# Finer interleaving of output products with attention, GpSimd's output work ordered after the causal masks, transposes one product later, and a third chain bank in an adaLN transformer block

## The chip, the core and the metric

The kernel runs on one core of one Trainium2 chip. The metric is device time in microseconds (us) for one execution. The core has five engines that run side by side, each through its own queue in order: TensorE (PE in the profile, with its weight loads as PEld) multiplies matrices into the accumulator memory PSUM, VectorE (DVE) and ScalarE (ACT) work element by element and can read PSUM, GpSimd (POOL) works element by element on the on-chip memory SBUF, and SyncE (SP) mostly issues DMA transfers. They wait for each other through semaphores.

## The reference

One adaLN-modulated transformer block in float32 on x of shape (2, 1024, 1024): two sequences ("batches"), 1024 tokens, model width 1024, 32 heads of 32, feed-forward width 2752.

```
mod = silu(c) @ wmod -> sa, ca, ga, sb, cb, gb          # |ga|, |gb| at least 0.25
h = layernorm(x) * (1 + ca) + sa
q, k, v = clip(h @ Wqkv.T, -8, 8)                       # then a layernorm over q and over k
scores = q k^T / sqrt(32) + slope_h * (pos_k - pos_q)   # causal
x = x + ga * (softmax(scores) v) @ Wout.T
h = layernorm(x) * (1 + cb) + sb
x = x + gb * ((silu(h Wg^T * ag) * (h Wu^T * au)) Wd^T * ad)
```

## The kernel before, in words

**Products in seven.** All large products use a Strassen-Winograd scheme on 2 x 2 blocks: seven block products in place of eight. For a pair of token tiles `j` (2 x 128 tokens), `seven` (L832) issues P1, P2, U2, P5, U3, P53, U6 in this order, each with four matmuls of 128x128 weights and 512 columns. (A float32 matmul shows as two records in the profile.) The operands are blocks (A11, ..) and sums of blocks (S1 to S4 of the tokens, T1 to T4 of the weights). S1 and S2 are made on VectorE, S3 and S4 on GpSimd (`sums_a`, L778); T1 and T2 on VectorE, T3 and T4 on GpSimd (L822 to L827). The seven go through two PSUM banks x and y, the chain: P1 goes into x, is copied out by ScalarE, and U2, U3 and U6 accumulate on it there; P2 goes into y and is read by VectorE, then P5 starts y anew, is copied out, and P53 accumulates on it. Each of P2, P53, U3 and U6 finishes a quarter of the result, which `read` takes out of the bank.

`Banks` (L745) hands out the banks. `pair` swaps x and y from one set of seven to the next. `turn` gives the next of the other banks for a transpose or a row-sum product. Where only one other bank is there, `fresh` says whether a step of the product has gone by since the last turn. In batch 0's projections there are four other banks, after that one.

**Between the matmuls.** After each `grain` matmuls `seven` yields, and the callback `between` may issue waiting pieces of work (`Todo`, L873): a layernorm's second half first, then transposes by TensorE of normalized token tiles (`turned`, L853: four 128x128 transposes into a bank, then copies out of it by VectorE, in batch 0's projections and the last output tiles shared with ScalarE), each with a `turn` of the banks. `places(q0, n)` says from which product on (`q0`) and how many at a place (`n`) transposes may go.

**Stages.** (1) The modulation vectors and batch 0's projections for q, k and most of v (`projections`, L943). Here a scheduler that estimates times may reorder TensorE's instructions. (2) Attention over both batches, with the rest as filler between its steps: the end of batch 0's v, batch 1's projections, then the output products of batch 0 and of batch 1's first half (`output`, L1265). From here on TensorE keeps the program's order (`pinned`), while the order on the other engines is still the scheduler's. (3) The output products of batch 1's second half, alone. (4) The feed-forward: gate and up products, then down products.

**Attention** (`attention`, L1022) goes through units of one group of four heads, one block of 512 queries and one block of 128 keys. `scores` issues four matmuls into four PSUM banks, ScalarE takes their exponentials (L1080), and where the key block touches the diagonal GpSimd zeroes what lies above it (the mask, `affine_select`, L1084). `weigh` multiplies with v two units later (`LAG`), and VectorE or GpSimd add the exponentials up (L1112). A `settle` makes row sums with a matrix of ones in one of the other banks (L1123, L1130). The four score banks are there once only, so the next unit's scores wait for this unit's exponentials.

**The weave.** `together` (L1157) takes attention's steps one by one and after each issues filler until the filler's share, by rough costs (`MM` = 0.9 us a matmul), stands level with attention. So the grain of the filler sets how finely the two are woven: it is 4 matmuls in batch 0's projections, 2 in batch 1's, and 2 in the output products.

**Output** works for each pair of token tiles on operands that `operand` (L1221) prepares during the product before: the attention result times the reciprocal row sums (L1246, half on VectorE and half on GpSimd), S1 and S2 on VectorE, S3 and S4 on GpSimd (L1250, L1251). `read` scales the result by ga (on GpSimd L1312, else VectorE) and adds it to x on GpSimd (L1313). Then comes the layernorm, the store of x by SyncE (L1320), the transposes, and `token_operands` (L1194), two of whose four subtractions are GpSimd's (L1201, L1202).

**The layernorm** (`normalize`, L696) takes statistics on VectorE, then 1/sqrt(var + eps) as exp(-0.5 ln) on ScalarE with one Newton step in tiny VectorE operations (L711, L719 to L722), and at last applies it (L724). `behind(a, b)` adds no wait: it tells the scheduler to put a after b.

Of the kernel before, what the change touches and what calls it, by code (L numbers as in the profile page):

```python
# [12 lines left out]
FP = mybir.dt.float32  # L13
# [6 lines left out]
P = 128  # L20
# [460 lines left out]
def kernel(  # L481
# [211 lines left out]
    last_exp = [None]  # L693
    last_mask = [None]

    def normalize(tiles, outs, small, nm):  # L696
# [12 lines left out]
        def rest_():  # L709
            ve = small.tile([P, n], FP, tag="ve", name=f"ve_{nm}")  # L710
            nc.vector.tensor_scalar_add(ve, mv[:, :, 1], EPS)  # L711
            lv = small.tile([P, n], FP, tag="lv", name=f"lv_{nm}")
            ln = nc.scalar.activation(lv, mv[:, :, 1], AF.Ln, bias=eps_t)
            if last_exp[0] is not None:
                behind(ln, last_exp[0])
            rstd = small.tile([P, n], FP, tag="rstd", name=f"rstd_{nm}")
            nc.scalar.activation(rstd, lv, AF.Exp, scale=-0.5)
            fix = small.tile([P, n], FP, tag="fix", name=f"fix_{nm}")
            nc.vector.tensor_mul(fix, rstd, rstd)  # L719
            nc.vector.tensor_mul(fix, fix, ve)  # L720
            nc.vector.tensor_scalar(fix, fix, -0.5, 1.5, ALU.mult, ALU.add)
            nc.vector.tensor_mul(rstd, rstd, fix)  # L722
            for m, (t, o) in enumerate(zip(tiles, outs)):
                nc.vector.tensor_scalar(o, t, mv[:, m, 0:1], rstd[:, m : m + 1], ALU.subtract, ALU.mult)  # L724
# [20 lines left out]
    class Banks:  # L745

        def __init__(self, two, others):
            self.two, self.others = two, others  # L750
            self.at = self.nt = self.made = 0
            self.seen = -1
            self.spare = None

        def pair(self):
            if self.spare is not None:
                x = self.two[self.at]
                self.two[self.at], self.spare = self.spare, x
            else:
                self.at ^= 1  # L760
            return self.two[self.at], self.two[1 - self.at]

        def fresh(self):
            return len(self.others) > 1 or self.made != self.seen

# [66 lines left out]
    def seven(a, bt, banks, read, between, grain):  # L832

        x, y = banks.pair()
        for c_, qa, qb_, q in SEVEN:
            bank = x if c_ == "x" else y
            first = q in ("P1", "P2", "P5")
            for j in range(KC // 2):
# [9 lines left out]
            banks.made += 1  # L848
            yield grain * MM
# [88 lines left out]
    def projections(b, pools, banks, places, extra=None, other=None, side=lambda n, e: None):  # L938
# [8 lines left out]
        for part in range(3):  # L947
            bt = weights_b(wp_, wqkv_t[:, ts(part, D)], f"{b}_{part}", wt_dram[part], other, b == 0 and part == 1)
            for j in range(NT // 2):
# [16 lines left out]
                part_t = {}  # L966
                q0, n = (2 - b, places) if b or part or j else (5, 4)

# [225 lines left out]
    def token_operands(b, j, h2, pool):  # L1194
# [24 lines left out]
    def operand(b, j, ap_):  # L1219
# [25 lines left out]
        for m, kh, q, eng in blocks:  # L1245
            eng.tensor_mul(a[q], a[q], rb[:, ds(kh * 4, 4), ts(m, P)])  # L1246
# [3 lines left out]
        nc.gpsimd.tensor_sub(a["S3"], a["A11"], a["A21"])  # L1250
        nc.gpsimd.tensor_sub(a["S4"], a["A12"], a["S2"])  # L1251
        made[b, j] = a
# [11 lines left out]

    def output(b, js, pools, banks, bt, todo, keep, q0=1, after=None):  # L1265

# [8 lines left out]
        for j in js:  # L1275
# [24 lines left out]
            def read(q, bank):  # L1300
# [9 lines left out]
                else:  # L1310
                    nc.vector.tensor_add(yg, yg, bank)
                    nc.gpsimd.tensor_mul(yg, yg, ga[:, ts(n, HALF)])  # L1312
                nc.gpsimd.tensor_add(xs[m][:, ts(n, HALF)], xs[m][:, ts(n, HALF)], yg)  # L1313
# [56 lines left out]
    with ExitStack() as st:  # L1370
# [77 lines left out]
        for us in dense0:  # L1448
            if us == "mark":
                break  # L1450
        banks.others = banks.others[0:1]
        banks.nt = 0
# [110 lines left out]
    def first_tokens():  # L1563
        ost.close()
        mid.close()
        banks.others.append(banks.spare)
        token_tiles((1, 0, 2, 3, 4, 6, 5))

    banks.spare = late_pools.enter_context(
        tc.tile_pool(name="spare_ps", bufs=1, space=PSUM, side="right")  # L1570
    ).tile([P, 512], FP, name="spare_ps")
    alone(output(1, range(NJ // 2, NJ), *out_args, 3, first_tokens))
# [370 lines left out]
```

## Time and profile before

| | us |
|---|---|
| median of three runs | 2319.51 |
| lowest and highest | 2312.93, 2321.79 |
| the profiled execution, its time | 2319.46 |
| the profiled execution, its span | 2317.7 |
| TensorE busy within the span | 2163.5 (93%) |
| VectorE, GpSimd, ScalarE busy | 1339.0, 1092.4, 945.9 |
| granted TensorE clock, mean | 0.979 |

How to read the lines below. A group of instructions is given as: line of the program, engine, operation, what it writes <- what it reads, shape, number of records | busy time in us, mean ns of one | the engine's idle time in us just before these instructions, and who ended it (<- engine, what it made, line). In the view by stretches of time each row has the stretch, its length, the busy time (and count) of PE, PEld, DVE, ACT and POOL, the granted TensorE clock as a share of full speed, the DMA share and GB/s. The timeline has start in us, duration in us, engine, line, operation, tiles, count, and in brackets the engine's idle time before it and who ended that.

### The profile page before, as it was taken

The numbers are of one execution on the slowest core, as the hardware profiler recorded it, in microseconds if no ns is written. First come the engines' busy times: TensorE is split into PE (matmuls) and PEld (weight loads), VectorE is DVE, ScalarE is ACT, GpSimd is POOL, SyncE is SP. The second block draws the span as 40 slices with busy tenths as digits, with TensorE's granted clock in tenths as the row PEclk, the third lists the DMA queues.
The fourth block names the chain that finished last, engine by engine and source line by source line (L and its number), as shares of the span: only waits on it lengthen the run. The fifth ranks groups of instructions, "written<-read, shape, count | busy, mean of one in ns | idle before, by whom it ended". The sixth has DMA issues, their size and how long they took to land. (4 is left out here: it accounts for less than half of the span.)

```text
span 2317.7 us, 27264 instructions
## 1 busy us (share of the span) xinstructions
PE 2163.5 (93%) x9537; PEld 1179.8 (51%) x9537; DVE 1339.0 (58%) x1843; ACT 945.9 (41%) x1782; POOL 1092.4 (47%) x775
## 2 busy tenths in 40 slices
PE   6999999999998899987898878999998999999998
PEld 2444443333333233332222234777776888788887
DVE  5775652455545643465656656877777554544445
ACT  1322224444444345555545514555454344323331
POOL 2330202443343563665666654577768777422212
PEclk9999999999999999999999989999999999999999
DMA  9887776446225431965343256767676786598765
GB/s 371 315 296 271 288 281 232 170 133 243 93 94 198 160 111 47 286 182 149 93 147 105 67 169 223 220 207 238 195 230 216 239 273 205 188 389 312 273 234 184
DMA packets 319350, 482.45 MB, mean 208 GB/s; under 512 B 16092, under 2 KB 235036, under 8 KB 310244
## 3 DMA queue, kind: packets, MB, share of 16 engines
q1 hardware_dynamic: 316752, 472.19, 60.5%
q10 hardware_dynamic: 2452, 8.43, 1.0%
q8 instruction: 77, 1.26, 0.2%
q14 instruction: 69, 0.57, 0.1%
HBM read 323.01 MB, written 157.55 MB: 207 GB/s over the span
## 5 line engine op out<-in xcount | busy, mean ns | idle before, releaser
L1080 ACT ACTIVATE p<-sc,kw 128x128 f32<-128x128 f32 (+3 forms) x1024 | 422.5, 515 | 419.6 <-PE sc L740 402.1
L740 PE MATMUL bank<-wT,a 128*128 128x512 f32 x768 | 367.3, 612 | 14.4 <-ACT P L972 7.9
L1112 POOL TENSOR_TENSOR p<-p,p 128x1024 f32<-128x1024 f32 (+3 forms) x128 | 263.5, 2059 | 220.8 <-PE av L740 193.9
L1112 DVE TENSOR_TENSOR p<-p,p 128x1024 f32<-128x1024 f32 (+3 forms) x192 | 237.2, 1248 | 123.0 <-POOL p L1084 66.6
L740 PE MATMUL bank<-wB,a 128*128 128x512 f32 x576 | 274.9, 614 | 1.3 <-DVE raw L979 0.7
L740 PEld LDWEIGHTS bank<-wT,a 128*128 128x128 f32 x768 | 137.0, 192 | 194.7 <-issue 161.7
L1084 POOL TENSOR_SCALAR_AFFINE_SELECT p<-p 128x256 f32<-128x256 f32 x256 | 135.9, 544 | 197.2 <-ACT p L1080 191.2
L740 PE MATMUL sc<-cq,ck 32*128 32x512 f32 (+3 forms) x1536 | 188.5, 534 | 26.8 <-ACT p L1080 26.6
L740 PE MATMUL av<-p,cv 128*32 128x512 f32 (+3 forms) x1536 | 169.6, 504 | 11.3 <-POOL p L1084 11.3
L740 PEld LDWEIGHTS bank<-wB,a 128*128 128x128 f32 x576 | 103.6, 192 | 148.0 <-issue 132.2
L1823 DVE TENSOR_TENSOR lo<-lo,hi 128x1408 fp32r<-128x1408 f32 x56 | 96.6, 1728 | 92.9 <-ACT hi L1822 92.9
L740 PEld LDWEIGHTS sc<-cq,ck 32*128 32x128 f32 x1536 | 63.9, 183 | 163.2 <-issue 92.5
L1822 ACT CAST hi<-lo 128x1408 fp32r<-128x1408 f32 x56 | 76.9, 1374 | 133.8 <-DMA lo<-act 79.9
L1887 POOL TENSOR_TENSOR early_P<-early_P,x1in 128x512 f32<-128x512 f32 x16 | 35.8, 2234 | 165.0 <-DVE early_P L1885 160.2
L979 DVE TENSOR_TENSOR raw<-P,bank 128x512 f32<-128x512 f32 x48 | 32.9, 684 | 126.8 <-PE bank L740 116.6
L740 PEld LDWEIGHTS av<-p,cv 128*32 128x32 f32 x1536 | 32.6, 109 | 137.0 <-issue 80.0
L740 PE MATMUL gy<-hs,wS 128*128 128x512 f32 (+1 forms) x352 | 89.1, 394 | 10.5 <-DVE gP L1739 4.8
L740 PE MATMUL gx<-hs,wS 128*128 128x512 f32 (+1 forms) x352 | 89.7, 397 | 6.8 <-ACT gU L1734 5.9
L740 PE MATMUL ux<-hs,wS 128*128 128x512 f32 (+1 forms) x352 | 89.9, 398 | 6.3 <-ACT uP L1734 5.8
L1632 POOL TENSOR_TENSOR wS<-wst,wst 128x1024 fp32r<-128x1024 f32 (+1 forms) x22 | 53.3, 2421 | 88.1 <-PE uy L740 70.1
L740 PE MATMUL ux<-hs,wA 128*128 128x512 f32 (+1 forms) x352 | 89.0, 394 | 2.7 <-DVE uP L1739 2.7
L740 PE MATMUL gx<-hs,wA 128*128 128x512 f32 (+1 forms) x352 | 89.3, 394 | 1.3 <-DVE hs L1548 1.2
(269 smaller groups left out, 3993.5 us busy)
## 6 DMA issues: line engine op xcount, KB each, us to landing
lo<-act SPq DMA_DIRECT2D x56, 704.0 KB
a<-hop SPq DMA_DIRECT2D x20, 1792.0 KB
wm<-in_L_wmod_dram SPq DMA_DIRECT2D x48, 512.0 KB
act<-aS SPq DMA_DIRECT2D x88, 256.0 KB
wB<-in_L_attn_Wqkv_dram SPq DMA_DIRECT2D x21, 1024.0 KB
wst<-in_L_ffn_Wg_dram SPq DMA_DIRECT2D x40, 512.0 KB
wst<-in_L_ffn_Wu_dram SPq DMA_DIRECT2D x40, 512.0 KB
qk<-qs SPq DMA_DIRECT2D x16, 1024.0 KB
```

The lines of the kernel that those rows point to most:

```text
L740: return in_order(nc.tensor.matmul(*args, **kw_))
L979: nc.vector.tensor_add(dst, part_t[MATE[q]], bank)
L1080: last_exp[0] = nc.scalar.activation(p[:, g, lo:hi], sp[:, g, lo:hi], AF.Exp, bias=kw[:, d, h_ : h_ + 1])
L1084: last_mask[0] = nc.gpsimd.affine_select(out=p[:, :, 0:P], in_=p[:, :, 0:P], pattern=[[0, 2], [1, P]], compare_op=ALU.is_ge, fill=0.0, bas ...
L1112: adders[b](half, jb).tensor_add(dst, dst, ps[half][:, :, 0:n])
L1632: nc.gpsimd.tensor_add(f["S1"], raw["A21"], raw["A22"])
L1822: nc.scalar.copy(hi, lo.bitcast(FP))
L1823: nc.vector.tensor_sub(lo, lo.bitcast(FP), hi.bitcast(FP))
L1887: eng.tensor_add(y, y, x1_of.pop(s))
```

## The change

Five edits.

1. `output` gives `seven` a grain of 1 beside attention (`q0 - 1` with `q0` now 2), and 2 as before in the last tiles. `Banks.made` counts matmuls instead of steps, and `fresh` with one other bank asks for more than one matmul since the last turn.
2. `masked` puts GpSimd's output work (L1201, L1202, L1246, L1250, L1251, L1312, L1313 of the kernel before) after the last mask issued so far, in the scheduler's order, while output runs beside attention.
3. Transposes may start from U2 instead of P2 (`q0` 2 instead of 1) in batch 1's projections and in output beside attention.
4. The chain may have three banks: `three` rotates a list, and P5 and P53 go into a bank z of their own. In batch 0's projections there are now three chain banks and three others (two and four before); beside attention two and one, as before, z then being y; in the last output tiles three, all in rotation, where a spare took turns with one of the two before. Two chain banks instead of the spare one go to the last transposes.
5. The layernorm's Newton step has four tiny VectorE operations instead of five, three instead of four of them after ScalarE's part.

```diff
+    beside = [False]
+
+    def masked(ins):
+        if beside[0]:
+            behind(ins, last_mask[0])
...
-            nc.vector.tensor_scalar_add(ve, mv[:, :, 1], EPS)
+            nc.vector.tensor_scalar(ve, mv[:, :, 1], EPS, -0.5, ALU.add, ALU.mult)
...
-            nc.vector.tensor_mul(fix, rstd, rstd)
-            nc.vector.tensor_mul(fix, fix, ve)
-            nc.vector.tensor_scalar(fix, fix, -0.5, 1.5, ALU.mult, ALU.add)
-            nc.vector.tensor_mul(rstd, rstd, fix)
+            nc.vector.tensor_mul(ve, ve, rstd)
+            nc.vector.tensor_mul(ve, ve, rstd)
+            nc.vector.scalar_tensor_tensor(rstd, ve, 1.5, rstd, ALU.add, ALU.mult)
...
-        def pair(self):
-            if self.spare is not None:
-                x = self.two[self.at]
-                self.two[self.at], self.spare = self.spare, x
-            else:
-                self.at ^= 1
-            return self.two[self.at], self.two[1 - self.at]
+        def three(self):
+            x, y = self.chain[0:2]
+            z = self.chain[-1]
+            self.chain = self.chain[1:] + [x]
+            return x, y, z
...
-            return len(self.others) > 1 or self.made != self.seen
+            return len(self.others) > 1 or self.made - self.seen > 1
...
-            bank = x if c_ == "x" else y
+            bank = x if c_ == "x" else y if q == "P2" else z
...
-                    banks.made += 1
+                    banks.made += grain
...
-                q0, n = (2 - b, places) if b or part or j else (5, 4)
+                q0, n = (2, places) if b or part or j else (5, 4)
...
-        nc.gpsimd.tensor_sub(t["T3"], b22, b12)
-        nc.gpsimd.tensor_sub(t["T4"], b21, t["T2"])
+        masked(nc.gpsimd.tensor_sub(t["T3"], b22, b12))
+        masked(nc.gpsimd.tensor_sub(t["T4"], b21, t["T2"]))
...
-            eng.tensor_mul(a[q], a[q], rb[:, ds(kh * 4, 4), ts(m, P)])
+            ins = eng.tensor_mul(a[q], a[q], rb[:, ds(kh * 4, 4), ts(m, P)])
+            if eng is nc.gpsimd:
+                masked(ins)
...
-    def output(b, js, pools, banks, bt, todo, keep, q0=1, after=None):
+    def output(b, js, pools, banks, bt, todo, keep, q0=2, after=None):
...
-            yield from seven(lambda q, i: a[q][:, i, :], bt, banks, read, todo.places(q0, 1, ahead), 2)
+            yield from seven(lambda q, i: a[q][:, i, :], bt, banks, read, todo.places(q0, 1, ahead), q0 - 1)
...
-        banks = Banks(three[0:2], three[2:3] + more[2:5])
+        banks = Banks(three[0:2] + more[4:5], three[2:3] + more[2:4])
...
+    beside[0] = True
     together(attention(apools, (halves, mostly), banks), dense_work(), share)
+    beside[0] = False
```

More of the change, by code (lines that the diff above doesn't have):

```diff
@@ L717, in rest_ @@
             nc.scalar.activation(rstd, lv, AF.Exp, scale=-0.5)
-            fix = small.tile([P, n], FP, tag="fix", name=f"fix_{nm}")
-            nc.vector.tensor_mul(fix, rstd, rstd)
-            nc.vector.tensor_mul(fix, fix, ve)
-            nc.vector.tensor_scalar(fix, fix, -0.5, 1.5, ALU.mult, ALU.add)
-            nc.vector.tensor_mul(rstd, rstd, fix)
+            nc.vector.tensor_mul(ve, ve, rstd)
+            nc.vector.tensor_mul(ve, ve, rstd)
+            nc.vector.scalar_tensor_tensor(rstd, ve, 1.5, rstd, ALU.add, ALU.mult)
             for m, (t, o) in enumerate(zip(tiles, outs)):
@@ L745, with __init__ @@
     class Banks:
[L749 to L753, printed above, removed]
-        def pair(self):
-            if self.spare is not None:
-                x = self.two[self.at]
-                self.two[self.at], self.spare = self.spare, x
-            else:
-                self.at ^= 1
-            return self.two[self.at], self.two[1 - self.at]
+        def __init__(self, chain, others):
+            self.chain, self.others = list(chain), others
+            self.nt = self.made = 0
+            self.seen = -2
+        def three(self):
[3 more added lines that the diff above has]
+            return x, y, z
         def fresh(self):
-            return len(self.others) > 1 or self.made != self.seen
+            return len(self.others) > 1 or self.made - self.seen > 1
         def turn(self):
@@ L832, in seven @@
     def seven(a, bt, banks, read, between, grain):
-        x, y = banks.pair()
+        x, y, z = banks.three()
         for c_, qa, qb_, q in SEVEN:
-            bank = x if c_ == "x" else y
+            bank = x if c_ == "x" else y if q == "P2" else z
             first = q in ("P1", "P2", "P5")
@@ L847, in seven @@
             read(q, bank)
-            banks.made += 1
+            banks.made += grain
             yield grain * MM
@@ L1249, in operand @@
         a["S3"] = a["A21"]
-        nc.gpsimd.tensor_sub(a["S3"], a["A11"], a["A21"])
-        nc.gpsimd.tensor_sub(a["S4"], a["A12"], a["S2"])
+        masked(nc.gpsimd.tensor_sub(a["S3"], a["A11"], a["A21"]))
+        masked(nc.gpsimd.tensor_sub(a["S4"], a["A12"], a["S2"]))
         made[b, j] = a
@@ L1311, in read @@
                     nc.vector.tensor_add(yg, yg, bank)
-                    nc.gpsimd.tensor_mul(yg, yg, ga[:, ts(n, HALF)])
-                nc.gpsimd.tensor_add(xs[m][:, ts(n, HALF)], xs[m][:, ts(n, HALF)], yg)
-            yield from seven(lambda q, i: a[q][:, i, :], bt, banks, read, todo.places(q0, 1, ahead), 2)
+                    masked(nc.gpsimd.tensor_mul(yg, yg, ga[:, ts(n, HALF)]))
+                masked(nc.gpsimd.tensor_add(xs[m][:, ts(n, HALF)], xs[m][:, ts(n, HALF)], yg))
+            yield from seven(lambda q, i: a[q][:, i, :], bt, banks, read, todo.places(q0, 1, ahead), q0 - 1)
             yield from todo.run(len(todo.list), True)
@@ L1450 @@
                 break
-        banks.others = banks.others[0:1]
+        banks.chain, banks.others = three[0:2], three[2:3]
         banks.nt = 0
@@ L1565, in first_tokens @@
         mid.close()
-        banks.others.append(banks.spare)
+        banks.others.extend(banks.chain[0:2])
         token_tiles((1, 0, 2, 3, 4, 6, 5))
-    banks.spare = late_pools.enter_context(
-        tc.tile_pool(name="spare_ps", bufs=1, space=PSUM, side="right")
-    ).tile([P, 512], FP, name="spare_ps")
+    spare = late_pools.enter_context(tc.tile_pool(name="spare_ps", bufs=1, space=PSUM, side="right"))
+    banks.chain.append(spare.tile([P, 512], FP, name="spare_ps"))
     alone(output(1, range(NJ // 2, NJ), *out_args, 3, first_tokens))
```

## The prediction

> **What bounds the kernel now.** I read the busy shares first, then busy time by stage, then the groups of TensorE instructions within a stage (their last column names what ended the idle time), then the timeline round the largest waits.
>
> ```profile
> PE 2163.5 (93%) x9537; PEld 1179.8 (51%) x9537; DVE 1339.0 (58%) x1843; ACT 945.9 (41%) x1782; POOL 1092.4 (47%) x775
> ```
> ```profile
> 0.00:361.00 361.00, 328.14 (x1062) 147.42 (x1062) 228.06 (x504) 85.57 (x197) 78.89 (x71) 0.99 0.81 301
> 361.00:930.00 569.00, 548.88 (x2579) 192.88 (x2578) 276.71 (x428) 253.68 (x623) 234.51 (x218) 0.98 0.42 145
> 930.00:1345.00 415.00, 361.51 (x2011) 117.62 (x2010) 244.78 (x334) 219.72 (x516) 263.33 (x237) 0.95 0.49 146
> 1345.00:1432.00 87.00, 74.88 (x199) 34.78 (x198) 54.42 (x93) 18.85 (x29) 49.19 (x32) 0.94 0.60 186
> ```
>
> Columns: stretch, its length, busy time of PE, PEld, DVE, ACT, POOL, granted clock, DMA. TensorE sets the pace, so only its waits can be won. Stage A (0 to 361) is batch 0's projections, B (361 to 930) attention with batch 1's projections beside it, C (930 to 1345) attention with output products beside it, D output alone. The change works in these four; the feed-forward after them has none of its edits. PE's idle time is 32.9, 20.1, 53.5 and 12.1 us. The groups of B, then of C:
>
> ```profile
> L743 PE MATMUL bank<-ident,raw 128*128 128x128 f32 x128 | 22.2, 299 | 17.9 <-DVE raw L724 15.9 <-DVE qs L860 2.0
> ```
> ```profile
> L740 PE MATMUL sc<-cq,ck 32*128 32x512 f32 (+3 forms) x736 | 95.4, 538 | 24.6 <-ACT p L1080 24.4
> L740 PE MATMUL av<-p,cv 128*32 128x512 f32 (+3 forms) x752 | 86.0, 510 | 11.3 <-POOL p L1084 11.3
> L740 PE MATMUL bank<-wB_o,aoA 128*128 128x512 f32 x96 | 49.9, 645 | 1.9 <-DVE oP L1309 1.9
> L743 PE MATMUL bank<-ident,xr 128*128 128x128 f32 x76 | 12.9, 294 | 15.7 <-DVE h2t L860 9.1 <-DVE xr L724 6.6
> ```
>
> Transposes wait for the layernorm (L724); in C scores wait for the exponentials of the unit before, weighing for the causal mask, transposes for their bank. One mask wait, GpSimd first, then TensorE:
>
> ```profile
> 1188.79 2.18 POOL L1312 TENSOR_TENSOR oP<-oP,ga 128x512 f32<-128x512 f32 x1 [1.76 <-DVE oP L1311]
> 1191.05 1.26 POOL L1313 TENSOR_TENSOR xr<-xr,oP 128x512 f32<-128x512 f32 x1
> 1192.27 1.26 POOL L1246 TENSOR_TENSOR aoA<-aoA,rb 128x512 f32<-128x512 f32 x1
> 1193.49 0.77 POOL L1084 TENSOR_SCALAR_AFFINE_SELECT p<-p 128x256 f32<-128x256 f32 x2
> ```
> ```profile
> 1193.95 1.86 PE L740 MATMUL av<-p,cv 128*32 128x384 f32 x8 [3.06 <-POOL p L1084]
> ```
>
> Three output operations stand ahead of the mask. So it is in all five mask waits (1.18, 0.85, 3.06, 2.53, 3.68 us): just before each stands L1246, L1312/L1313 or L1202/L1250.
>
> A wait costs more than itself: the granted clock falls to half afterwards.
>
> ```profile
> 575.00:585.00 10.00, 7.84 (x33) 3.25 (x32) 7.26 (x17) 2.04 (x8) 2.18 (x2) 0.83 0.23 96
> 710.00:720.00 10.00, 4.98 (x16) 2.08 (x16) 8.84 (x9) 0.68 (x2) 4.34 (x2) 0.66 0.00 1
> ```
>
> After a wait of 2.16 us at 578 the mean over 10 us is 0.83, 1.7 us of clock lost; after 6.89 us at 715 it is 0.66, 3.4 us. B has two of each, 10.2 us. In C the 50-us rows from 1000 to 1350 read 0.97, 0.94, 0.95, 0.90, 1.00, 0.97 and 0.90: 18.5 us.
>
> **The change part by part.** The sum is made against the profiled execution's 2319.46 us (span 2317.7 and 1.8 around it), which equals the median of the three runs, 2319.51. Orders of instructions are those of the two built programs.
>
> *B, transposes a product later.* The four waits are 2.16, 1.70, 6.89 and 6.89 us. Stage B's 569 us hold about 98 products, 5.8 us each; at 715 the work that now comes first is half of P2 (1.98), weighing 1.07, scores 1.14, half of U2 (1.98): 6.2 us. VectorE meanwhile gets one or two more additions (1.22 each), so I leave 2 us of each long wait; the 2.16 goes, the 1.70 (a bank still being read) stays. Gain 12. Three half-clock windows of 1.7 remain: 10.2 - 5.1 = 5 more. Bounds: from a loss of 2 (a crowded bank, the price of the 1.70 once more) to all of it gained, 28. I take 17, since the row at 715 shows the work that fills the hole. With the transposes move their four VectorE copies (0.40 each) and the stores of queries and keys on SP's queue, which leave up to 5.8 us later; attention on batch 1 reads them only after the value projections, so that is hidden; without this cover it is 5.8 us once.
>
> *Shorter layernorm.* One VectorE operation fewer per call, 0.16 us alone, but next to GpSimd's additions the same small operation took 2.31 and 2.29 us (L721, L722 at 706 and 710). It lies before the waits of B and helps there to hold the 2 us; elsewhere I count 0.5 us.
>
> *C, products singly.* ScalarE needs 4 x 0.605 us for a 512-wide unit (87.3 us over 144), 0.50, 0.39 and 0.28 each for narrower ones; counting what TensorE has to do between one unit's scores and the next in both orders (0.96 us a product matmul, 1.07 a 512-wide unit), the shortfalls add up to 38.6 us before and 28.1 after. The trace's wait is 24.4, so scaled by 0.73 it becomes 17.8: gain 6.6. Against it the product blocks go from 77 to 142; a block's last matmul starts its successor 522 ns later where one inside a block takes 430, so 65 x 0.09 = 6 us lost. Bounds of the two together: -15 to +8; I take -0.6.
>
> *C, GpSimd's output work behind the masks.* The five waits are met, 11.3 us. But in the new order each output's four operand operations (L1246 twice, L1250, L1251: 1.46, 1.46, 1.69, and 2.28 in the one row I looked at) mostly stand together ahead of the next masks, some 6.9 us, where they were spread. Six such runs lie in C. A mask is used two units after its scores, 2 x 4.5 us, less 2.4 for exponentials and some 2 for an addition on GpSimd: slack 4.6, so up to 2 us each; I take 0.8, 5 together. Gain 6.3, bounds -11.3 and +8. Behind an output operation that waits stand GpSimd's own additions (L1112), whose sums are needed at the end of a head group and whose reading frees one of six p buffers. Who waits for the delayed operations: x1's stores on SP (64.7 us of waiting in C already, longest 15.3), with loads of operands and attention chunks queued behind. Chunks are asked for two groups ahead, operands a product ahead; this is the cover, a rival below prices its loss.
>
> *C, transposes.* The 6.6 us on L724 go (a product lasts 10 us here). The 9.1 on L860 stays, less a little; new are two places where a row-sum product follows a transpose in its bank with 0 and 1.3 us of work between, 2 us each. Gain 4.5, bounds -15 and +5.
>
> *C, clock.* Waits fall from 53.5 to about 36, and the deep ones most; I take 18.5 to 10, gain 8.5, bounds 0 and 18.5.
>
> C together: -0.6 - 6.3 - 4.5 - 8.5 = -20.
>
> *A, third chain bank, one bank fewer for transposes.* P5 no longer waits for P2's reader: 2.23 us at 109, and 1.25 at 316 to 321 between two products. The 4.13 at 152 is U6 behind U3's reader, same bank still, and stays. But the first product is reordered: P5 before U2, and on GpSimd S3 and S4 now stand behind eight weight sums:
>
> ```profile
> 43.62 6.28 POOL L825 TENSOR_TENSOR wT<-wB,wB 128x512 f32<-128x512 f32 x4 [5.55 <-DMA wB<-in_L_attn_Wqkv_dram]
> 49.86 5.58 POOL L827 TENSOR_TENSOR wT<-wB,wT 128x512 f32<-128x512 f32 x4
> ```
>
> These end at 55.4; S3 and S4 (1.27 each) at 58.0; then eight matmuls of 0.86 end P53 at 64.9, where it ends at 62.2 now: 2.7 lost, and 1.7 of clock. Net of A +1, bounds -4 and +10 (transposes on three banks wait 0.3 us today).
>
> *D.* The same products; chain rotation and a third bank for the last transposes touch waits of 0.4 and 1.6 us: 0, bounds -3 and +3.
>
> Sum: -17 - 0.5 - 20 + 1 = -36.5, so 2283.
>
> **A rule against a row.** TensorE: Matmul & The Clock Gate, Part 1 (HAM oscillation) says that the clock falls only after idle gaps over some 3.4 us. The trace disagrees: 2.16 us idle was followed by 3.4 us at half clock. By the page the clock terms of B and C would be 6.8 and 5.1 instead of 5 and 8.5, and the sum about 2285 (an estimate).
>
> **The rivals.** (1) *The weave gives nothing*: runs of GpSimd operations and crowded banks take back all of C (bounds above reach +13), B alone gains: 2303. For it: POOL is busy 263 of 415 us in C. Against it: the scores' and masks' waits have their causes in rows. (2) *Nothing comes of it*: B's transposes wait a product later as long as before, since VectorE's queue sets the layernorm: 2319. Against it: L724 let TensorE go at 715.0 after a chain of VectorE operations that waited for nothing of TensorE's after 708. (3) *Operands late*: behind masks, the operand multiplications reach TensorE too late. D shows the price of one, 6.7 us on L1246 at 1369 and 3.4 of clock, 10.1; six operands in C make 61 and 2344. They have some 7 single matmuls, 17 us, from issue to use; from four late ones on the gain is gone, from five it is a loss beyond 0.5%.
>
> **How the numbers follow.** Forecast 0.68, its own range 2256 to 2300; rival 1 0.16 (2296 to 2312); rival 2 0.08 (2308 to 2326); rival 3 0.08. A measurement of this kernel tells about 0.5% from no change, 2308 to 2331. Faster: 0.68 and most of rival 1, 0.81; same 0.10; slower 0.09. The range, 2256 to 2312, leaves out rivals 2 and 3 and a little below: 0.2.
>
> **What would show it.** Stage B near 550 us, its transposes' wait on L724 under 5 us; C near 395, scores' wait under 19, mask waits under 6 and none behind L1312; a new wait for GpSimd at 55 to 58 us; granted clock in C over 0.96. Wrong would be: waits on the operands' L1246 line in C, or stores of x1 that hold back attention chunks.

## The result

The changed kernel takes 2332.63 us (median of 15 runs, 2325.48 to 2340.75) where the kernel before takes 2319.51 (median of 15 runs beside it): a ratio of 1.0056, 95% interval 1.0041 to 1.0071. It was to become 1.6% faster and became 0.6% slower. The profiled execution has a span of 2332.6 us, against 2317.7 before.

Four moments on TensorE cut the span: the first scores (end of A), the first output product (end of B), the last weighing with v (end of C) and the last output matmul (end of D). A grew from 361.4 to 369.3 us, B shrank from 575.1 to 563.5, C grew from 406.1 to 419.1, D from 88.9 to 93.3. That is +7.9 - 11.6 + 13.0 + 4.4 = +13.7 of the 14.9 us; the feed-forward has the rest.

Busy time by stage after, in the columns explained above (stretch, length, PE, PEld, DVE, ACT, POOL, granted clock, DMA):

```profile
0.00:369.00 369.00, 331.04 (x1062) 148.93 (x1062) 220.71 (x488) 85.80 (x197) 80.35 (x71) 0.97 0.80 295
369.00:933.00 564.00, 551.72 (x2610) 193.11 (x2610) 282.21 (x427) 256.91 (x632) 237.72 (x220) 0.99 0.43 149
933.00:1352.00 419.00, 361.64 (x1967) 106.79 (x1967) 236.34 (x315) 215.66 (x506) 260.13 (x234) 0.94 0.46 140
1352.00:1445.00 93.00, 77.06 (x208) 34.91 (x208) 60.55 (x96) 19.35 (x30) 49.13 (x32) 0.96 0.57 177
```

C of the kernel before, cut by the same moments:

```profile
936.00:1343.00 407.00, 353.51 (x1976) 114.89 (x1976) 239.56 (x325) 216.33 (x507) 260.78 (x232) 0.95 0.49 146
```

In C TensorE is both busier (361.6 against 353.5 us) and idler (57.4 against 53.5). TensorE's groups that waited, first B's transposes, then three of C:

```profile
L746 PE MATMUL bank<-ident,raw 128*128 128x128 f32 x128 | 21.4, 291 | 10.1 <-DVE qs L860 9.8 <-DVE raw L727 0.2
```
```profile
L743 PE MATMUL sc<-cq,ck 32*128 32x512 f32 (+3 forms) x720 | 95.2, 561 | 34.2 <-ACT p L1080 31.4 <-DMA ck<-qk 2.0
L743 PE MATMUL av<-p,cv 128*32 128x512 f32 (+3 forms) x744 | 84.1, 510 | 11.1 <-POOL p L1084 11.1
L746 PE MATMUL bank<-ident,xr 128*128 128x128 f32 x76 | 13.3, 301 | 8.2 <-DVE h2t L860 8.2
```

B's wait on the layernorm (15.9 us, L724 before, L727 now) is gone, as forecast; but the transposes now wait 9.8 us for their own bank (L860), where they waited 2.0. In C the mask waits did not move (11.3 and 11.1), and the scores' waits on exponentials rose from 24.4 to 31.4, the longest from 2.8 to 10.0 us. The timeline at that longest wait, without TensorE's weight loads and DMA issues:

```profile
1126.40 1.27 ACT L1080 ACTIVATE p<-sc,kw 128x512 f32<-128x512 f32 x2 [2.59 <-PE sc L743]
...
1126.96 2.94 POOL L1246 TENSOR_TENSOR aoA<-aoA,rb 128x512 f32<-128x512 f32 x2
...
1131.13 1.77 POOL L1252 TENSOR_TENSOR aoA<-aoA,aoA 128x512 f32<-128x512 f32 x1 [1.23 <-DVE aoS L1249]
1132.86 1.26 POOL L1253 TENSOR_TENSOR aoS<-aoA,aoS 128x512 f32<-128x512 f32 x1
1134.08 0.77 POOL L1084 TENSOR_SCALAR_AFFINE_SELECT p<-p 128x256 f32<-128x256 f32 x2
1134.52 0.60 DVE L1112 TENSOR_TENSOR p<-p,p 128x256 f32<-128x256 f32 x1 [2.74 <-POOL p L1084]
...
1135.04 0.68 DVE L1311 TENSOR_TENSOR oP<-ga,bank 128x512 f32<-128x512 f32 x1
1135.79 1.26 POOL L1315 TENSOR_TENSOR xr<-xr,oP 128x512 f32<-128x512 f32 x1
1137.09 0.69 DVE L711 BATCH_NORM_STATS2 st_f<-xr 128x6 f32<-128x512 f32 x1 [1.38 <-POOL xr L1315]
1137.82 0.21 DVE L712 BATCH_NORM_AGGREGATE mv_f<-st_f 128x2 f32<-128x12 f32 x1
1138.06 0.30 ACT L718 ACTIVATE lv_f<-mv_f,eps_t 128x2 f32<-128x2 f32 x1 [10.40 <-DVE mv_f L712]
...
1138.50 1.25 ACT L1080 ACTIVATE p<-sc,kw 128x512 f32<-128x512 f32 x2
...
1139.80 2.08 PE L743 MATMUL sc<-cq,ck 32*128 32x512 f32 x4 [10.02 <-ACT p L1080]
```

Read it from below. The scores wait for exponentials. ScalarE has half of a unit's exponentials done at 1127.7, and next in its queue stands the layernorm's logarithm (Ln, L718), unready for 10.4 us. It needs the statistics. These need the last addition into x1 on GpSimd (L1315), and that needs the reading of U6's bank on VectorE (L1311). In VectorE's queue a sum of exponentials (L1112) stands ahead of this reading, and it waits for a mask. The mask stands on GpSimd behind four operand operations of the next tile pair (L1246 twice, L1252, L1253), 1126.96 to 1134.1. ScalarE's waits on Ln in C, before and after (total, times, longest):

```profile
ACT lv_f L713 <- DVE mv_f L707: 5.8, 2, 5.5
```
```profile
ACT lv_f L718 <- DVE mv_f L712: 36.4, 5, 10.4
```

### The profile page after: what moved, and what is told of

Same layout as the page of the kernel before. It is cut to its first block, busy times and chain, and to the rows that moved or that the text cites. A ratio compares the mean times of both kernels' runs of the same rounds, so it can differ in the third digit from the quotient of the medians.

```text
span 2332.6 us, 27239 instructions
## 1 busy us (share of the span) xinstructions
PE 2172.1 (93%) x9537; PEld 1171.4 (50%) x9537; DVE 1335.0 (57%) x1811; ACT 946.0 (41%) x1782; POOL 1097.0 (47%) x775
## 4 chain that ended last, share of the span: by engine, by line
PE 33%; POOL 9%; DVE 4%; issue 4%; DMA 3%; ACT 2%; SPq 0%; POOLq 0%; DVEq 0%; ACTq 0%
PE dx L743 7%; PE dy L743 5%; PE ux L743 4%; PE gx L743 4%; PE uy L743 3%; PE gy L743 3%; PE bank L743 3%; POOL aS L1710 2%; PE sc L743 2%; DVE p L1112 1%; DMA wdst<-in_L_ffn_Wd_dram 1%; ACT p L1080 1%; POOL xr L1315 1%; DMA wst<-in_L_ffn_Wu_dram 1%; PE av L743 1%
## 5 line engine op out<-in xcount | busy, mean ns | idle before, releaser
L1112 POOL TENSOR_TENSOR p<-p,p 128x1024 f32<-128x1024 f32 (+3 forms) x128 | 263.9, 2062 | 240.6 <-PE av L743 215.4
L743 PE MATMUL bank<-wT,a 128*128 128x512 f32 x664 | 318.3, 612 | 6.4 <-DVE raw L979 4.3
L1112 DVE TENSOR_TENSOR p<-p,p 128x1024 f32<-128x1024 f32 (+3 forms) x192 | 247.3, 1302 | 110.1 <-POOL p L1084 57.2
L743 PE MATMUL bank<-wB,a 128*128 128x512 f32 x496 | 235.3, 608 | 0.9 <-DVE raw L977 0.8
L743 PE MATMUL sc<-cq,ck 32*128 32x512 f32 (+3 forms) x1536 | 190.9, 546 | 36.4 <-ACT p L1080 33.6
L743 PEld LDWEIGHTS bank<-wT,a 128*128 128x128 f32 x664 | 118.6, 192 | 165.1 <-issue 147.0
L743 PE MATMUL av<-p,cv 128*32 128x512 f32 (+3 forms) x1536 | 169.8, 507 | 11.1 <-POOL p L1084 11.1
L743 PEld LDWEIGHTS bank<-wB,a 128*128 128x128 f32 x496 | 87.5, 189 | 128.6 <-issue 118.4
L743 PE MATMUL ux<-hs,wS 128*128 128x512 f32 (+1 forms) x352 | 88.5, 393 | 4.7 <-ACT uP L1737 4.1
L743 PE MATMUL uy<-hs,wS 128*128 128x512 f32 (+1 forms) x352 | 88.8, 394 | 2.5 <-DVE uP L1742 2.5
```

The source lines that it names most:

```text
L743: return in_order(nc.tensor.matmul(*args, **kw_))
L1112: adders[b](half, jb).tensor_add(dst, dst, ps[half][:, :, 0:n])
```

## The experiments

The ratio is to the kernel before, timed on the same chip; its median there was 2321.3 to 2323.2 us. Stage lengths in us are from one profiled execution each. Compare runs by the ratio: the medians come from different chips.

| run | ratio, 95% interval | A | B | C | D |
|---|---|---|---|---|---|
| before | 1 | 361.4 | 575.1 | 406.1 | 88.9 |
| changed | 1.0056 (1.0041 to 1.0071) | 369.3 | 563.5 | 419.1 | 93.3 |
| e1_no_masks | 1.0010 (0.9998 to 1.0022) | 369.9 | 564.6 | 410.6 | 94.3 |
| e2_two_banks | 1.0029 (1.0013 to 1.0045) | 361.5 | 564.5 | 419.1 | 93.0 |
| e3_pairs | 0.9928 (0.9909 to 0.9947) | 371.5 | 563.5 | 396.3 | 95.2 |
| e4_later_alone | 0.9962 (0.9945 to 0.9978) | 364.6 | 565.9 | 404.3 | 86.8 |
| e5_singles_late | 1.0021 (1.0010 to 1.0033) | 371.8 | 564.7 | 412.7 | 91.8 |
| e6_pairs_no_masks | 0.9929 (0.9914 to 0.9944) | 370.7 | 563.3 | 393.0 | 94.9 |
| e7_pairs_two_oldd | 0.9916 (0.9897 to 0.9935) | 361.9 | 564.3 | 393.1 | 94.6 |
| e8_later_both | 0.9912 (0.9897 to 0.9927) | 361.3 | 567.6 | 389.2 | 95.0 |
| e9_singles_bare | 1.0006 (0.9997 to 1.0016) | 370.3 | 564.5 | 404.3 | 94.5 |
| e10_last_early | 0.9917 (0.9901 to 0.9933) | 365.2 | 567.6 | 396.2 | 89.0 |
| e11_short_ln | 0.9986 (0.9974 to 0.9998) | 361.8 | 571.2 | 406.5 | 88.8 |
| e12_ln_in_d | 0.9907 (0.9892 to 0.9922) | 364.6 | 562.5 | 395.9 | 86.2 |
| e13_three_for_transposes | 0.9953 (0.9936 to 0.9971) | 364.8 | 564.3 | 389.3 | 94.6 |
| e14_four_then_third | 0.9922 (0.9905 to 0.9940) | 365.6 | 561.9 | 398.3 | 88.5 |

### What costs C: the ordering, the split, or both

My first theory blamed the ordering behind the masks; the rival was the split into single products. e1_no_masks takes away the first, e3_pairs the second.

```diff
-    beside[0] = True
```

> The changed kernel without the ordering of GpSimd's output work behind the masks; all else stays. Theory M (the ordering delays the last additions into x1, so that the layernorm's Ln stands unready in ScalarE's queue between the exponentials of one unit): ScalarE's waits on lv_f in the stage with output products beside attention fall from 36.4 us to under 12, the two waits of 10.0 and 5.8 us of the scores and the 5.7 us mask wait go together with about 10 us of half clock; some 10 us of small mask waits come back. That stage falls from 419 to about 400 us and the time from 2332.6 to about 2314. Rival S (the split into single products costs it): the stage stays at 415 to 420 us and the time at 2329 to 2334.

```diff
-todo.places(q0, 1, ahead), q0 - 1)
+todo.places(q0, 1, ahead), 2)
```

> The changed kernel with output products in pairs beside attention instead of singly, everything else kept (masks, later transposes). Theory M: the late Ln stays, so the stage beside attention stays within 6 us of 419 us; the scores' ordinary waits rise by about 7 us, the cadence gives 6 back; time 2328 to 2338. Rival S (singles cost it): the stage falls to about 405 us and the time to about 2318.

Without the ordering the kernel takes 2325.9 us, with pairs 2306.7. So the ordering costs something (C 8.5 us shorter without it, Ln's waits 17.1 instead of 36.4), but the rival is far larger: with pairs C falls by 23 us though the ordering stays, and Ln's waits fall to 6.8. My theory had missed that the grain also decides *when* the layernorm's second half and the operands are issued: both go out at the first place in a product, which with singles comes one matmul in and with pairs two. Two more runs separate this place, the ordering and the split itself. The first is e5_singles_late; `hold` is 1 after an output product beside attention.

> The changed kernel, output products still singly, but the layernorm's second half and the next product's operand multiplications are issued after two single matmuls, where the pairs have them, not after one. Theory P (two causes: the split itself costs 13 us of TensorE's busy time, 0.2 us for each of the 65 further blocks, and the early place of Ln and operands costs another 13 of waiting): the waits on lv_f fall from 36.4 to under 12 us, the stage beside attention from 419 to about 406, the time by 13 to about 2320; product matmuls stay at about 177 us busy. Rival (the split alone): the stage stays over 415. Rival (the place alone): the stage falls to 396 to 400.

```diff
                 side(order.index(q))
+                if self.hold:
+                    self.hold -= 1
+                    return
                 self.place()
...
                 elif e == 6 and step and nxt not in made:
-                    next(step[0])
+                    seen.append(e)
+                    if len(seen) == (2 if q0 == 2 else 1):
+                        next(step[0])
```

The second, e9_singles_bare, is the same without the ordering behind the masks.

> Output products singly, with neither the ordering behind the masks nor the early place of Ln and operands: the split alone on top of what pairs without the ordering have (393.0 us beside attention, 2308). Theory P: the 65 further blocks cost TensorE 9 to 10 us of busy time (mean of six stages 342 against 332 without the half clock), less 5 for the scores' shorter waits, so the stage is at 398 to 403 us and the time at about 2315. Rival (the place and the ordering were all of it): the stage is at 390 to 394 and the time at about 2308. Rival (the split costs far more than its blocks): the stage stays over 408 and the time over 2322.

The later place alone (e5) gives 2328.1 us and C 412.7, between the two theories; Ln still waits 21 us, since the ordering holds the additions back. With neither ordering nor early place (e9) Ln's waits are 7.6 us, the time is 2323.2 and C 404.3, more than I expected. This is the split alone, to be compared with pairs without the ordering (the edits of e1 and e3 together):

> Pairs beside attention, and GpSimd's output work not ordered behind the masks; the rest as changed. Theory: the ordering gains nothing in pairs either, since mask waits were 15.7 us with it against 11.3 before; the stage stays within 4 us of 396 and the time within 5 us of the pairs' 2306.7. Rival (the ordering gains what was forecast): mask waits rise by 6 us, the stage to 404 or more, the time to 2314.

e6 takes 2308.3 us. Busy time of C in e9 (singles), then in e6 (pairs):

```profile
935.00:1339.00 404.00, 359.40 (x1966) 105.71 (x1965) 243.08 (x314) 214.94 (x506) 262.35 (x232) 0.96 0.48 145
```
```profile
934.00:1327.00 393.00, 346.60 (x1966) 111.84 (x1964) 238.78 (x313) 215.06 (x506) 260.69 (x232) 0.96 0.50 149
```

The same work at the same mean clock keeps TensorE busy 12.8 us longer in singles. A stage's length has three parts: TensorE's busy time as it would be at full clock, its idle time, and what half clock adds while TensorE runs (half of the busy time inside such stretches). Half clock that falls into idle time adds nothing. From the traces, C comes apart like this, in us:

| | before | changed | e9, singles | e6, pairs | e8, see below |
|---|---|---|---|---|---|
| busy, at full clock | 335.2 | 344.2 | 347.6 | 332.5 | 333.0 |
| idle | 53.5 | 57.4 | 44.6 | 46.4 | 46.9 |
| added by half clock | 17.4 | 17.5 | 12.1 | 14.1 | 9.2 |

In the five runs in singles (changed, e1, e2, e5, e9) the first row is 344.2 to 347.6, on average 345.6; in the eight in pairs with later transposes in C it is 330.7 to 333.0, on average 332.4. So the split costs some 13 us of busy time. Where this comes from stands in the starts of the blocks. The timeline of before, a pair (four records) and its successor; then of the changed kernel, a single and its successor:

```profile
1237.78 1.98 PE L740 MATMUL bank<-wT_o,aoS 128*128 128x512 f32 x4
1239.69 1.14 PE L740 MATMUL sc<-cq,ck 32*128 32x512 f32 x8
```
```profile
1127.60 1.12 PE L743 MATMUL bank<-wB_o,aoA 128*128 128x512 f32 x2
1128.66 1.13 PE L743 MATMUL sc<-cq,ck 32*128 32x512 f32 x4
```

A pair holds TensorE for 1.91 us, two singles for 2 x 1.06 = 2.12. Over C's undisturbed blocks at full clock, on average: the pair's four records start their successors after 526, 429, 429 and 522 ns (67 blocks of before, sum 1906), a single's two after 530 and 521 (108 blocks after, sum 1050). Both the first and the last record of a block cost about 95 ns more than one inside. A split adds one of each, 0.19 us, and 65 splits make 12.6 us. Next to transposes, whose tile is 128x128 as well, the edge costs nothing: in A of before (60 to 360 us) 32 products before a transpose took 429 ns and 31 transposes before a product 109, as within their own kind. The other neighbours in C of before agree: from scores to weighing, two shapes, the last 512-column record starts its successor after 517 ns (17 places), from row sums to weighing, one shape, after 409 (7 places). It is the change to another tile shape that costs: 32x128 for scores, 128x32 for weighing and row sums. The Trainium skill says so (TensorEngine Tiling (Array Packing), Tiling Modes, Key Properties): a change of tiling mode, not of the tile alone, drains TensorE. It gives no price; the price here is 95 ns an edge.

What singles were to gain they did gain: the scores' waits on exponentials are 17.5 us in e9 and 25.6 in e6. But waits of transposes and row sums on the bank, 11.8 us against 4.4 in e6, eat it, among them the one that the prediction named, a row-sum product right behind a transpose in its bank. The timeline of the changed kernel:

```profile
1252.98 0.66 PE L746 MATMUL bank<-ident,xr 128*128 128x128 f32 x4
1257.45 1.51 PE L743 MATMUL bank<-p,ones 128*32 128x512 f32 x8 [3.81 <-DVE h2t L860]
```

So the split by itself turns a ratio of 0.9929 (e6) into 1.0006 (e9), some 18 us, and the ordering with the early place adds the rest up to 1.0056, some 12. How these two share it is not settled. In singles the profiles of C give the ordering 8.5 us (with the early place) or 8.4 (without), and the early place 6.4 or 6.3. The ratios give either alone little (1.0021 for the ordering, 1.0010 for the early place) and most to both together. In pairs the ordering does nothing either way: e3 and e6 differ by 0.0001 in the ratio, and mask waits are 15.7 us with it and 14.2 without.

### What the later transposes give

```diff
-                q0, n = (2 - b, places) if b or part or j else (5, 4)
+                q0, n = (2, places) if b or part or j else (5, 4)
```

> The kernel before with nothing but the transposes of batch 1's projections a product later. Theory: the gain of 11.6 us that attention on batch 0 showed is this edit's alone; that stage falls from 575 to about 563 us and the time from 2319.5 to about 2308. Rival (the gain needed the shorter layernorm, or is handed back at the hand-over to the output stage): time 2314 to 2320.

The time falls to 2313.7 us, 8.8 us by the ratio, and B to 565.9. The group of transposes in B of this run (e4_later_alone):

```profile
L743 PE MATMUL bank<-ident,raw 128*128 128x128 f32 x128 | 20.9, 286 | 12.2 <-DVE qs L860 10.9 <-DVE raw L724 1.3
```

14.6 us of the wait on the layernorm go and 8.9 come back as waits on the bank. I take it that transposes now follow each other closer in the one bank; no run shows this by itself.

```diff
 as e4, and
-    def output(b, js, pools, banks, bt, todo, keep, q0=1, after=None):
+    def output(b, js, pools, banks, bt, todo, keep, q0=2, after=None):
```

> The kernel before with the transposes a product later in batch 1's projections and in the output products; pairs, chains, layernorm and GpSimd's order as before. Theory: all that the changed kernel gains is in this edit; attention on batch 0 about 565 us, the stage with output products about 396 (before 406), the time 2319.5 - 10 - 10 = about 2300. Rival (in the output stage the gain needs the ordering behind the masks or the shorter layernorm): that stage stays at 403 to 407 and the time at about 2311.

2303.1 us, 20 us by the ratio, and C at 389.2, better than expected. One number in two places gives as much as any combination of the change's edits did. Stages B, C and D of this run (e8_later_both):

```profile
361.00:929.00 568.00, 553.54 (x2610) 193.16 (x2609) 285.55 (x435) 256.80 (x631) 238.88 (x222) 0.99 0.43 148
929.00:1318.00 389.00, 342.07 (x1964) 110.39 (x1964) 239.55 (x318) 215.45 (x506) 259.88 (x232) 0.97 0.51 151
1318.00:1413.00 95.00, 79.03 (x212) 35.81 (x211) 61.16 (x101) 19.55 (x30) 50.13 (x33) 0.91 0.59 175
```

The shorter layernorm alone (the change's fifth edit on the kernel before):

> The kernel before with nothing but the shorter layernorm. Theory: one small VectorE operation less for each call is hidden nearly everywhere; the time is within 3 us of before's 2319.5 to 2322.5. Rival (it shortens the waits of transposes on the layernorm, 17.9 us beside attention on batch 0): 5 to 8 us faster.

2317.8 us, 0.14% below before, at the edge of what these runs tell; B is 3.9 us shorter and its wait on the layernorm 13.3 instead of 15.9 (the 17.9 of the expectation holds 2.0 on the bank).

### The start of batch 0

```diff
-        banks = Banks(three[0:2] + more[4:5], three[2:3] + more[2:4])
+        banks = Banks(three[0:2], three[2:3] + more[2:5])
```

> The changed kernel with batch 0's chain of two banks and four others, as before. Theory: S3 and S4 of the first product go before the eight weight sums again on GpSimd, the waits of 5.8 us at 44 and 6.3 us at 60 go, the first scores start at about 362 instead of 369.3, and the time falls by 8 us to about 2324.7. Rival (the later start only shifts a wait on the loads or the weights): first scores at 367 or later, time within 2 us of 2332.6.

A is back at 361.5 us, and the ratio falls by 0.0027, 6 us where 8 were expected. The timeline of the changed kernel at its start shows the loss:

```profile
44.05 6.45 PE L743 MATMUL more<-wT,a 128*128 128x512 f32 x8 [5.82 <-DVE a L783]
50.34 3.60 PE L743 MATMUL bank<-wT,a 128*128 128x512 f32 x8
60.27 2.08 PE L743 MATMUL more<-wB,a 128*128 128x512 f32 x2 [6.34 <-POOL a L786]
62.14 4.16 PE L743 MATMUL bank<-wT,a 128*128 128x512 f32 x8
66.14 2.74 PE L743 MATMUL more<-wB,a 128*128 128x512 f32 x6
```

P5 waits for S1 (L783) and P53 for S4 (L786); the first tile's P53 ends at 68.9 where it ended at 62.3. Is it the third chain bank, which lets P5 go ahead, or the fourth transpose bank, which it takes away?

For e13 the chain begins with two banks and the others with three, and at the second tile the bank that neither had, `more[4]`, joins the chain. For e14 the others begin with four and hand one over:

> Pairs without the ordering behind the masks (2308.3, first scores at 370.7 us), where the first output tile has a chain of two banks and three others for transposes, and the third chain bank comes from the second tile on. Theory Q (the start is late because the first tile's fourth transposed block finds only three banks and waits for a reader, so that all of S1 to S4 go behind the weight sums): the waits on S2 or S1 at 44 us and on S4 at 60 us stay and the first scores are at 368 or later. Rival (the start is late because a third chain bank lets P5 go ahead of U2): the first scores are at 360 to 363 and the time at about 2300.

```diff
-        banks = Banks(three[0:2] + more[4:5], three[2:3] + more[2:4])
+        banks = Banks(three[0:2], three[2:3] + more[2:5])
...
+                if (b, part, j) == (0, 0, 1):
+                    banks.chain.append(banks.others.pop())
```

> The first output tile has two chain banks and four for transposes, from the second tile on three and three; besides, pairs, no ordering behind the masks, the last tile's transposes early and Ln behind the copy of P1's bank in the stage of output alone. Theory Q: S3 and S4 go ahead of the weight sums again, nothing of the late start remains, and the third bank takes away the wait of 2.2 us at 109: first scores at 358 to 361 us; the whole about 2 us under the 2299.2 of the best so far. Rival (three banks for transposes cost elsewhere in that stage what the third chain bank gains): first scores at 362 to 366, the time at 2299 to 2303.

TensorE's idle time in A says it more steadily than the lengths: 32.9 us before and 32.5 to 33.4 in all runs whose first tile has two chain banks and four for transposes, 35.5 in e13, 37.4 to 38.9 in those with the third bank from the start. So each is about half of it: with three banks the fourth transposed block waits for a reader, and S1 to S4 are made behind the weight sums (e13 waits 8.6 us at 47, but only 1.9 at 59); with the third chain bank P5 and P53 then wait in turn as well. Neither theory holds alone. Later the third bank is worth nothing: in e14 the wait at 109 is gone (1.9 to 2.2 us in the runs with two), but 1.1 us at 112 and 1.6 at 328 have come, and A's idle time is 33.2. In time the later third bank shows no gain either: the ratio of e13 is 0.9953, above e6's 0.9929 though its profile (the fastest of its six runs) has a shorter A, and that of e14 is 0.9922, above e12's 0.9907 below.

### Output alone, and the best kernel

Pairs, two banks at the start and the old rotation (e7_pairs_two_oldd):

> Pairs beside attention, batch 0's chain of two banks, and in the stage of output alone the chain as before (one bank alternating with the spare, P5 in the bank of P2). Theory: against the pairs' 2306.7 the start gains 6 to 8 us and output alone, 95.2 us with three in rotation and 87 to 89 without, gains 6: about 2293. Rival (the longer stage of output alone comes from the order of work on GpSimd and VectorE, not from the banks): that stage stays at 93 or more and the time near 2299.

```diff
+            if len(self.chain) > 2:
+                self.chain = self.chain[::-1]
+                return self.chain[0], self.chain[1], self.chain[1]
```

The start's gain comes in A (361.9 us), D's does not come: 94.6 us with the old rotation. The time is 2302.6 us, not 2293, and by the ratio 3 us under e3's. D is long in e8 too, which has the chains of before. So in pairs the rotation is not its cause. ScalarE in D of e8 (the row of TensorE is from the same timeline):

```profile
1353.36 0.29 ACT L713 ACTIVATE lv_f<-mv_f,eps_t 128x2 f32<-128x2 f32 x1 [16.24 <-DVE mv_f L707]
...
1353.79 0.57 ACT L1303 COPY oP<-spare_ps 128x512 f32<-128x512 f32 x1
...
1354.41 2.93 PE L740 MATMUL spare_ps<-wT_o,aoS 128*128 128x512 f32 x3 [8.94 <-ACT oP L1303]
```

The same thing as in C: an unready Ln in ScalarE's queue, here ahead of the copy of P1's bank, and U2 waits 8.9 us. Two cures were tried. The first, on top of e8:

```diff
-todo.places(q0, 1, ahead), 2)
+todo.places(1 if (b, j) == (1, NJ // 2 - 1) else q0, 1, ahead), 2)
```

> The kernel before with both transposes a product later (2303.1), but the last output tile that begins beside attention keeps its transposes at the early place. Theory: output alone was 95.0 us there against 86.8 with early transposes, since four transposes fall into it and a copy of P1's bank on ScalarE stood 16.2 us behind an unready Ln, for which TensorE waited 8.9 us; with the early place the stage is back at 87 to 89 and the time at about 2296. Rival (the wait comes from GpSimd's order there and stays): the stage at 93 or more, the time within 2 us of 2303.

D falls to 89.0 us as expected, but the time stays at 2303.1: C is 7 us longer in this run, of which 4.4 are added by half clock (13.6 instead of 9.2), and the median shows no gain. The three runs with this edit (e10, e12, e14) have C at 395.9 to 398.3 us, e8 and e13 at 389.2 and 389.3: it seems to move the cost from D to C, and no run shows why.

The second cure keeps that edit, takes the shorter layernorm, and in D issues the layernorm's second half at the third place of the next product instead of at once (`hold` is 2) and puts Ln behind the copy of P1's bank:

```diff
+                    copied = nc.scalar.copy(part_t[q], bank)
+                    if q0 == 3:
+                        last_exp[0] = copied
```

> As the run with the last tile's transposes early, with the shorter layernorm too, and in the stage of output alone ScalarE's Ln is issued behind the next tile's copy of P1's bank, not ahead of it. Theory (an unready Ln in ScalarE's queue holds up what stands behind it): TensorE's waits on ScalarE's copies there, up to 8.9 and 2.5 us, go, the stage falls to 80 to 85 us and the time to about 2290. Rival (TensorE then waits as long for the operands' multiplication or for a bank's reader): the stage stays at 87 to 89 and the time at about 2296.

2299.2 us, 0.93% below before and the lowest ratio of all, though the intervals of e7, e8, e10 and e14 overlap with its own. ScalarE in its D (e12_ln_in_d):

```profile
1350.27 0.58 ACT L1304 COPY oP<-spare_ps 128x512 f32<-128x512 f32 x1
1354.63 0.29 ACT L713 ACTIVATE lv_f<-mv_f,eps_t 128x2 f32<-128x2 f32 x1 [3.78 <-DVE mv_f L707]
```

Ln now waits behind the copy and holds nobody up; what TensorE waited for on ScalarE's copies is gone, but a wait of 6.2 us on the operand's multiplication on GpSimd (L1247 there) remains, as large as in e4 and e10. D is 86.2 us, not 80 to 85. Against e10 the medians differ by 4 us with overlapping intervals, so what Ln's place alone gains stays unsettled; it is tried together with the shorter layernorm.

## Why the prediction was wrong

Two steps failed and turned C from -20 to +13 us. The price of the finer weave was put at one edge of each block instead of two: at full clock TensorE is busy 9.0 us longer in C than before, and some 13 longer than in pairs. The list of who waits for the delayed operations left out the layernorm's Ln on ScalarE, which held the scores, so idle time in C rose by 3.9 us where 17 were to go. A smaller step was to count half clock as lost also where TensorE is idle.

**B, transposes a product later: -17 forecast, -11.6 found** with the shorter layernorm (-9.2 alone in e4, -3.9 for the layernorm alone in e11). The mechanism is right: L724 lets go nearly at once. The term that was mis-sized is the bank: I left 2 us of each long wait and kept one wait of 1.70, and five waits of 9.8 us in all stand there instead. So idle time fell by 7.8 us, not 12. The clock's part was 4.1 us (7.3 added by half clock before, 3.2 after), not 5.

**Shorter layernorm: -0.5 forecast, about -3 found**, nearly all in B. I counted 0.5 us outside B and put its help in B into the term above.

**C, products singly: -0.6 forecast, +11 in the profile of C and some 18 us by the ratios found.** Here the forecast turned. The gain in the scores' waits was about right (8.1 us; forecast 6.6). "a block's last matmul starts its successor 522 ns later where one inside a block takes 430" was right too, but only half of the price: the block's *first* record costs as much (526 ns), and the rows of before show it. So the price is 65 x 0.19 instead of 65 x 0.09, some 13 us instead of 6. The other half of the error is the bank: I gave two places behind a transpose 2 us each and booked them under the transposes, and e9 has 7.4 us more of such waits than e6.

**C, GpSimd's output work behind the masks: -6.3 forecast, 0 in pairs, a loss in singles.** The failed step is "Who waits for the delayed operations: x1's stores on SP". That list left out the reader that mattered: x1's additions feed the layernorm's statistics, and its Ln stands in ScalarE's in-order queue among the exponentials. The profile of before had the row, 5.5 us on lv_f in C; with the ordering and the early place these waits became 36.4 us, and one of them held the scores for 10.0. The runs of operand operations ahead of the masks, which I did foresee, took back the masks' own gain.

**C, transposes: -4.5 forecast, too low.** e8 is 15.1 us shorter in C than e4, e10 is 8.1; their difference is mostly half clock. Of e8's 15.1 only 5.5 are idle time: the transposes' wait is 4.6 us where it was 15.7, but mask waits rose from 10.4 in e4 to 14.4. Another 7.0 are added by half clock, of which e10 keeps 2.6.

**C, clock: -8.5 forecast, nothing found**, since the waits did not shrink. Counted as the prediction counts, over all of C, the clock lost rises from 18.3 to 24.8 us. But half clock can begin inside a wait, where it costs nothing. So it was at the prediction's own example, the wait that ends at 715.0 in before, and at the longest wait after (TensorE idle, then busy again; the granted clock is the third number from the end):

```profile
708.10:715.00 6.90, 0.03 (x4) 0.00 (x0) 6.86 (x5) 2.42 (x4) 6.16 (x3) 0.79 0.23 83
715.00:718.80 3.80, 3.78 (x8) 1.92 (x8) 3.19 (x6) 0.00 (x0) 0.00 (x0) 0.50 0.00 0
```
```profile
1129.80:1139.80 10.00, 0.00 (x0) 0.00 (x1) 5.29 (x12) 1.65 (x4) 5.85 (x7) 0.59 0.38 113
1139.80:1145.30 5.50, 5.50 (x18) 1.72 (x22) 1.04 (x2) 3.01 (x5) 0.00 (x0) 0.50 0.92 176
```

The wait at 715 cost 1.9 us of clock, not 3.4, and the one at 1139.8 2.8 us of the 6.8 that its stretch lost. Over C half clock added 17.4 us before and 17.5 after; with the right parts alone (e8) it is 9.2.

**A: +1 forecast, +7.9 found.** I named the late S3 and S4, from the order of instructions, but priced the end of P53 at 2.7 us later. It is 6.5: VectorE's S1 and S2 also went behind weight sums, and I had put the wait at 44 us nowhere. The gain of 2.23 and 1.25 at the third bank came back as other waits.

**D: 0 forecast, +4.4 found.** In pairs four more transposes fall into D and an unready Ln holds up a copy. The changed kernel itself keeps its number of transposes in D; its rows show 2.6, 4.8 and 2.8 us on VectorE's reading of chain banks, late behind statistics that wait for GpSimd, and what shifts them there was not taken apart.

**The rivals.** The third came nearest, with the wrong victim: GpSimd's work was late, but not for TensorE, where no wait on L1246 appears in C. Of the other sign, attention chunks held back by stores of x1, there is a wait of 2.0 us for one chunk (ck), but no store of x1 stands in SyncE's queue from 950 to 974 us, just ahead of it. The first, that the weave gives nothing and B alone gains, had the right doubt with an end of 2303; it did not go on to ask what each further block costs at both edges.

## What to carry to other kernels

Price a finer interleaving by both edges of each further block where the tile shape changes (here 0.19 us a split), before counting what waits it fills. For an operation that is put back on one engine, follow its readers until an in-order queue of another engine is reached, and look what stands behind the first reader there; a tiny Ln held the scores for 10 us in this way. Split a stage's length into busy time at full clock, idle time and what half clock adds while the engine runs, before putting a price on the clock. Where several edits go together, run the one with the simplest mechanism alone: one number in two places gave more than all five edits.

## What the runs showed of the hardware

The half clock after the same waits varies from run to run. Before, e2, e4, e7, e8, e10, e11 and e12 share the start of batch 0 (two chain banks, four others), and TensorE is idle there for 32.5 to 33.4 us in all of them. But round the wait that ends at 45 to 47 us the clock stands at half for 6.8 us in before, e2, e7, e8 and e11 and for 10.2 us in e4, e10 and e12. The stretch begins inside the wait and ends 3.0 to 4.1 us after it in the former, 4.6 to 6.2 us in the latter. Round the wait of some 3 us at 297 it stands at half for 6.8 us in e4 and e12, 3.4 in e10 and not at all in the others. In all, half clock adds 3.2 to 3.8 us to A in the former and 7.0 to 8.2 in the latter, and the first scores lie at 361.3 to 361.9 and at 364.6 to 365.2. So 3 us of difference in A say nothing about an edit.
